# A planned graph-attention and GGNN kernel: seven durations in the plan's cost table are edited

## The chip, the cores and the metric

The kernel runs on one core of one Trainium2 chip. The metric is the device time of one execution in microseconds, as a median over the executions shown. TensorE (PE), VectorE (DVE), ScalarE (ACT), GpSimd (POOL) and the DMA queue of SyncE (SP) each run their own list of instructions; semaphores hold an instruction back until what it needs is done.

## What is computed

The input is x of 128 graphs x 128 nodes x 256 features, with an adjacency matrix of 128 x 128 for each graph. Four residual layers follow each other. The first three are graph attention (GAT), the last is a gated graph network of three steps (GRU):

```python
h = relu(layernorm(x))
# layers 0, 1, 2
Wh = h @ W
e = leaky_relu((Wh @ a1)[:, :, None] + (Wh @ a2)[:, None, :], 0.2)
att = softmax(where(adj > 0, e, -9e15))
x = x + elu(att @ Wh)            # layer 2: times nodemask ahead of elu
# layer 3, three steps i
m = h @ weight[i]
aggr = A.T @ m                   # A = (adj != 0)
h = gru_cell(aggr, h, w_ih, w_hh, b_ih, b_hh)
x = x + h
```

## The kernel before

**Groups.** The 128 graphs are cut into 33 groups: group 0 and group 32 have two graphs, the others four, so that a tile of a group is 128 partitions x 512 columns. A group passes through three attention layers and then through three GRU steps. While PE works on the GRU steps of group g, the attention layers of groups g+1 to g+3 are in progress, so that their long chains of DVE, ACT, POOL and DMA work lie beside matmuls of another group.

**Matmuls.** All are in float32, and the trace shows two MATMUL records for each product (transposes have one). An attention layer has the products `ahp` (L627: weights times nodes, four of 128 columns for each of two halves) and `hp` (L646, 256 columns). A GRU step has, for each half c of the features, products of 512 columns into four banks, `nn`, `r`, `z`, `ni` (L790): six from the state h and the recurrent weights, six from the aggregate `ag` and the combined weights. The aggregate itself is `agp` (L813: four products of 128 columns for each half k, from the node-major state `hn` and the adjacency `am`).

**Chains.** After `agp` of half k, ACT copies the bank to `ag` (L821), and the products of `ag` can start. After the last `r`, `ni` and `z` products of half c, ACT and DVE make the new state: tanh of r (L848), n (L851, L856), tanh (L858), d (L871 or L873, L877), h (L880). The next step's products read that h. For groups 2 to 30 the node-major copy `hn` of h is made with a DVE transpose (L476) and two DMA passes through DRAM (L479, L483); the others turn it on PE (`hnp`, L762, and an ACT copy, L802).

**Banks.** PSUM is dealt out in rings: two banks for `ahp` and `hp` (tag gat), five for the GRU products (gru), and one bank for `agp`, `hnp` and `hTp` (tag tr). An `agp` can thus begin only when ACT has copied out whatever was put into that single bank before it.

**What sets the order.** No order is written out by hand, and none is found at run time. Every operation is given to a planner (class Plan, L39 on) with an engine, a cost in microseconds and a rank (a due time in units of a group's third). The planner runs through the whole kernel once while it is built: an engine is free again when an operation's cost has passed, a result reaches another engine after a further LAG (0.26 from PE, 0.2 from DVE and ACT), a DMA lands after a time of its own, and a ring's slot comes free when its last user ends. At each step, for the engine that can start first, it takes from the operations that could start within WINDOW = 0.1 of the earliest the one of lowest rank. The result is one list for each engine, which the chip then executes in that order, whatever the true durations are:

```python
first = min(t for t, _ in found)
soon = [(op.rank, t, i) for i, (t, op) in enumerate(found) if t <= first + self.WINDOW]
_, t, i = min(soon)
```

The costs come from small functions: pe(cols) (L259), dve(cols) = 0.12 + cols/1000, act(cols) = 0.25 + cols/1400, and from numbers beside single operations. pe(128) is the cost of an `agp` or `ahp` product, that is of two MATMUL records. A cost is used by the planner alone: no instruction depends on it except through its place in its engine's list, and through the buffers that go with that order.

Of the kernel before, what the change touches and what calls it, by code (L numbers as in the profile page):

```python
# [14 lines left out]
P = 128  # L15
# [24 lines left out]
class Plan:  # L40
# [21 lines left out]
    def add(self, engine, cost, rank, fn, reads=(), writes=(), after=(), takes=()):  # L62


        reads = [k if isinstance(k, tuple) else (k, None) for k in reads]
        writes = [k if isinstance(k, tuple) else (k, None) for k in writes]
        vals = list(dict.fromkeys(v for v, _ in reads + writes))
        vals += [v for v in dict.fromkeys(takes) if v not in vals]
        op = Op(engine, cost, rank, fn, vals)
        for v in vals:  # L70
            v.ops.append(op)

        def others(book, key):
            for part, ops in book.get(key[0], {}).items():
                if part is None or key[1] is None or part == key[1]:
                    yield from ops

        for key in reads:
            for d in others(self.writers, key):
                op.deps[d] = True  # L80
        for key in writes:
            for book in (self.writers, self.readers):
                for d in others(book, key):
                    op.deps.setdefault(d, False)
        for d in after:
            op.deps.setdefault(d, False)
        for v, part in writes:
            w, r = self.writers.setdefault(v, {}), self.readers.setdefault(v, {})
            if part is None:
                w.clear()  # L90
                r.clear()
            else:
                r.pop(part, None)
            w[part] = [op]
        for v, part in reads:
            if (v, part) not in writes:
                self.readers.setdefault(v, {}).setdefault(part, []).append(op)
        for d in op.deps:
            d.users.append(op)
        self.ops.append(op)  # L100
        return op
# [84 lines left out]
def kernel(  # L186
# [25 lines left out]
    nc = tc.nc  # L212
    B, N, D = x.shape
# [44 lines left out]
        )  # L258

    def pe(cols):  # L260
        return 0.035 + cols / 600 if cols <= P else 0.01 + cols / 600

    def dve(cols):
        return 0.12 + cols / 1000
# [149 lines left out]
    def stats(xt, n, name, rank, takes):  # L414

        st = val(gw, "st", [G, 6], f"st_{name}", cut=n)
        mv = val(gw, "mv", [G, 2], f"mv_{name}", cut=n)
        nm = val(gw, "nm", [G], f"nm_{name}", cut=n)
        ve = val(gw, "ve", [G], f"ve_{name}", cut=n)
        rs = val(gw, "rs", [G], f"rs_{name}", bufs=3, cut=n)  # L420

        def one(b):
            add("DVE", dve(D), rank, lambda: nc.vector.bn_stats(st.t[:, b, :], xt.t[:, b, :]),
                reads=[(xt, b)], writes=[(st, b)], takes=[mv, nm, ve, rs, *takes])
            add("DVE", 0.13, rank, lambda: nc.vector.bn_aggr(mv.t[:, b, :], st.t[:, b, :]),
                reads=[(st, b)], writes=[(mv, b)])

        for b in range(n):
            one(b)
        add("DVE", 0.16, rank, lambda: nc.vector.tensor_scalar(  # L430
            nm.t, mv.t[:, :, 0], -1.0, None, op0=OP.mult), reads=[mv], writes=[nm])
        add("POOL", 0.3, rank, lambda: nc.gpsimd.tensor_scalar(
            ve.t, mv.t[:, :, 1], EPS, None, op0=OP.add), reads=[mv], writes=[ve])
        add("POOL", 1.04, rank, lambda: nc.gpsimd.tensor_tensor(
            rs.t, ve.t, mhalf[:, :n], op=OP.pow), reads=[ve], writes=[rs])
        return nm, rs
# [54 lines left out]
    def attention(g, l, xt, cap, xo):  # L491
# [5 lines left out]
        far = g >= FAR  # L497
# [6 lines left out]
                reads=[nm, rs], writes=[nm])  # L504

        def centred(b):
            add("ACT", 0.45, rank, lambda: nc.scalar.activation(  # L507
                xn.t[:, b, :], xt.t[:, b, :], AF.Relu, bias=nm.t[:, b : b + 1],
                scale=rs.t[:, b : b + 1] if far else 1.0,
            ), reads=[(xt, b), nm, *([rs] if far else [])], writes=[(xn, b)])  # L510


        def score(b, s):
            scr = val(gw, "scr", [D], f"scr_{name}_{b}_{s}")
            add("DVE", dve(D), rank, lambda: nc.vector.scalar_tensor_tensor(  # L515
                scr.t, xn.t[:, b, :], 1.0 if far else rs.t[:, b : b + 1], VA[l].t[:, s, :],
                op0=OP.mult, op1=OP.mult, accum_out=e.t[:, s, b : b + 1],
            ), reads=[(xn, b), rs, VA[l]], writes=[scr, (e, (s, b))])
# [53 lines left out]
            nmx.t, em.t, axis=AX.X, op=OP.max, negate=True), reads=[em], writes=[nmx])  # L572

        def power(b):
            add("ACT", 0.42, rank, lambda: nc.scalar.activation(  # L575
                em.t[:, b, :], em.t[:, b, :], AF.Exp, bias=nmx.t[:, b : b + 1],
                accum_out=sm.t[:, b : b + 1],
            ), reads=[(em, b), nmx], writes=[(em, b), (sm, b)])
# [4 lines left out]
        if l == 2:  # L583
            add("DVE", 0.16, rank, lambda: nc.vector.tensor_mul(
                ri.t, ri.t, nmT.t[:, FIRST[g] : FIRST[g] + n]), reads=[ri, nmT], writes=[ri])
        add("DVE", dve(n * P), rank, lambda: nc.vector.tensor_tensor(
            em.t, em.t, ri.t.rearrange("p (g o) -> p g o", o=1).to_broadcast([P, n, N]), op=OP.mult
        ), reads=[em, ri], writes=[em])

# [80 lines left out]
    def gat(g):  # L670
        b0, n = FIRST[g], SIZES[g]
        rank = 3.0 * g - lead(g)
        x0 = xt = val(grp, "x0", [G, D], f"x_{g}", cut=n)
        adj_t = val(grp, "adj", [G, N], f"adj_{g}", dtype=I32, cut=n)
        cap = val(grp, "cap", [G, N], f"cap_{g}", cut=n)
        am = val(grp, "am", [G, N], f"am_{g}", bufs=4, cut=n)
        load(128 * n, rank - 4, lambda: nc.sync.dma_start(
            x0.t, x[b0 : b0 + n].rearrange("b n d -> n b d")), writes=[x0])
        load(64 * n, rank - 3.6, lambda: nc.sync.dma_start(
            adj_t.t, adj[b0 : b0 + n].rearrange("b i j -> i b j")), writes=[adj_t])  # L680
        add("DVE", 0.42, rank, lambda: nc.vector.tensor_scalar(
            cap.t, adj_t.t, 0.0, 2.0 * BIG, op0=OP.is_gt, op1=OP.mult), reads=[adj_t], writes=[cap])
        add("DVE", 0.42, rank, lambda: nc.vector.tensor_scalar(
            cap.t, cap.t, -BIG, None, op0=OP.add), reads=[cap], writes=[cap])
        add("DVE", 0.42, rank + 1, lambda: nc.vector.tensor_scalar(
            am.t, adj_t.t, 0.0, None, op0=OP.not_equal), reads=[adj_t], writes=[am])
        for l in range(3):
            xo = val(grp, f"x{l + 1}", [G, D], f"xo_{g}_{l}", bufs=3 if l == 2 else 2, cut=n)
            attention(g, l, xt, cap, xo)
            xt = xo  # L690
        rank = 3.0 * g - lead(g) + 5.5
        hn = val(grp, "hn0", [G, D], f"hn_{g}_0", cut=n)

        F = KD * n * 32
        hT = val(grp, "h0", [Q, KD * G * 32], f"h_{g}_0")
        nm, rs = stats(xt, n, f"{g}_3", rank, [hn, hT])
        add("DVE", 0.16, rank, lambda: nc.vector.tensor_mul(nm.t, nm.t, rs.t),
            reads=[nm, rs], writes=[nm])

        def normed(b):  # L700
            add("ACT", 0.45, rank, lambda: nc.scalar.activation(
                hn.t[:, b, :], xt.t[:, b, :], AF.Relu, bias=nm.t[:, b : b + 1],
                scale=rs.t[:, b : b + 1],
            ), reads=[(xt, b), nm, rs], writes=[(hn, b)])

        for b in range(n):
            normed(b)

        def turned(k):

            ps = bank("tr", f"hTp_{g}_{k}")

            def turn(b):
                add("PE", 0.11, rank, lambda: nc.tensor.transpose(
                    ps.t[:, b * P : (b + 1) * P], hn.t[:, b, k * P : (k + 1) * P], ident
                ), reads=[(hn, b)], writes=[(ps, b)], takes=[hT])

            for b in range(n):
                turn(b)
            add("ACT", act(n * P), rank, lambda: nc.scalar.copy(  # L720
                hT.t[:, :, :F].rearrange("p q (k b c) -> p k b q c", k=KD, b=n)[:, k],
                ps.t[:, : n * P].rearrange("p (b q c) -> p b q c", b=n, q=Q),
            ), reads=[ps], writes=[(hT, k)])

        if g == 0:
            for k in range(KD):
                turned(k)
            return xt, am, hn, hT

        exchanged(  # L730
            [hn] * KD, lambda k: hn.t[:, :, k * P : (k + 1) * P], hT, f"h_{g}", n, rank
        )
        return xt, am, hn, hT
# [235 lines left out]
```

## Time and profile before

| | us |
|---|---|
| median of three executions | 2757.75 |
| lowest, highest | 2756.5, 2758.16 |
| the profiled execution, its own time | 2757.73 |
| span in the profile, first to last instruction | 2756.0 |
| PE busy (matmul records) | 2712.8 |
| DVE busy | 2082.3 |
| ACT busy | 1280.4 |
| POOL busy | 293.7 |

The profiled execution lies at the median of the three, and 1.7 us of its time lie outside the span. The mean granted clock of TensorE is 0.996 of full speed. Matmuls overlap in their pipeline, so that a record is longer than the distance to the next: a 128x512 matmul is recorded with 594 ns and followed by the next after 430 ns.

### The profile page before, as it was taken

Reading aid. Unit: us, or ns where it says so; the run is one execution under the profiler, and the core shown is the slowest. Engines: PE = TensorE matmul, PEld = TensorE weight load, DVE = VectorE, ACT = ScalarE, POOL = GpSimd, SP = SyncE. Lnnn points to the kernel's source line nnn. Section 1 sums busy time; section 2 is a strip of 40 time slices with the busy share of each in tenths; the row PEclk is TensorE's granted clock in tenths of the full one; section 3 lists DMA queues with packets and bytes.
Section 4 is the critical chain, followed back from the end, with each engine's and each line's share of the span. In section 5 each row is a group of like instructions: output and inputs, shape, how many; then the busy total and the mean of one; then the engine's idle time right before and its main releaser. Section 6 shows DMA issues by size and latency. Waiting matters only on the chain.

```text
span 2756.0 us, 32248 instructions
## 1 busy us (share of the span) xinstructions
PE 2712.8 (98%) x9563; PEld 1569.7 (57%) x9563; DVE 2082.3 (76%) x5541; ACT 1280.4 (46%) x2709; POOL 293.7 (11%) x369
## 2 busy tenths in 40 slices
PE   7899999999999999999999999999999999999998
PEld 4755555555555555555555555555555555555546
DVE  7778888778768887877788687778768886876643
ACT  4545444444444454444454445444444444444433
POOL 1111110101101101110111111111101010100000
PEclk9999999999999999999999999999999999999999
DMA  3113334433324433333333344323334333333310
GB/s 91 51 58 100 88 95 101 111 94 86 97 80 108 108 99 78 101 91 96 105 97 83 87 105 104 109 75 91 97 88 110 103 93 86 94 74 93 79 44 12
DMA packets 503094, 245.30 MB, mean 89 GB/s; under 512 B 280580, under 2 KB 472068, under 8 KB 502919
## 3 DMA queue, kind: packets, MB, share of 16 engines
q1 hardware_dynamic: 502918, 243.25, 33.5%
q8 instruction: 76, 1.25, 0.2%
q14 instruction: 100, 0.81, 0.1%
HBM read 139.28 MB, written 103.87 MB: 88 GB/s over the span
## 4 chain that ended last, share of the span: by engine, by line
PE 88%; DVE 8%; ACT 2%; DMA 1%; issue 1%; POOL 0%; SPq 0%; DVEq 0%; ACTq 0%; POOLq 0%
PE z L790 21%; PE r L790 21%; PE hp L646 11%; PE ni L790 11%; PE nn L790 10%; PE ahp L627 6%; PE agp L813 5%; DVE em L557 1%; DVE scr L515 1%; DVE xo L662 1%; DVE xo L664 1%; DVE d L877 1%; ACT em L575 1%; DVE h L880 1%; DVE n L856 0%
## 5 line engine op out<-in xcount | busy, mean ns | idle before, releaser
L790 PE MATMUL nn<-h,whh 128*128 128x512 f32 (+1 forms) x792 | 395.6, 581 | 1.9 <-DVE h L880 1.9
L790 PE MATMUL r<-ag,wc 128*128 128x512 f32 (+1 forms) x792 | 395.2, 581 | 1.3 <-ACT ag L821 1.3
L790 PE MATMUL ni<-ag,wc 128*128 128x512 f32 (+1 forms) x792 | 394.4, 579 | 1.4 <-ACT ag L821 1.4
L790 PE MATMUL z<-ag,wc 128*128 128x512 f32 (+1 forms) x792 | 394.2, 579 | 0.0
L790 PE MATMUL z<-h,whh 128*128 128x512 f32 (+1 forms) x792 | 394.2, 579 | 0.0
L790 PE MATMUL r<-h,whh 128*128 128x512 f32 (+1 forms) x792 | 394.2, 579 | 0.0
L851 DVE SCALAR_TENSOR_TENSOR n<-r,wn 128x512 f32<-128x512 f32 (+1 forms) x198 | 132.6, 670 | 336.5 <-ACT r L848 336.0
L646 PE MATMUL hp<-w,ah 128*128 128x256 f32 x1536 | 373.2, 381 | 0.5 <-ACT ah L634 0.2
L646 PEld LDWEIGHTS hp<-w,ah 128*128 128x128 f32 x1536 | 290.1, 190 | 131.4 <-issue 95.7
L515 DVE SCALAR_TENSOR_TENSOR scr<-xn,va 128x256 f32<-128x256 f32 x732 | 266.4, 423 | 33.9 <-ACT xn L507 33.6
L848 ACT ACTIVATE r<-r,brz 128x512 f32<-128x512 f32 (+1 forms) x198 | 133.2, 673 | 284.3 <-PE r L790 282.0
L813 PEld LDWEIGHTS agp<-am,hn 128*128 128x128 f32 x1536 | 202.3, 191 | 85.7 <-issue 73.5
L790 PEld LDWEIGHTS ni<-ag,wc 128*128 128x128 f32 x792 | 149.8, 190 | 177.9 <-issue 171.0
L790 PEld LDWEIGHTS r<-h,whh 128*128 128x128 f32 x792 | 149.3, 190 | 169.4 <-issue 162.8
L790 PEld LDWEIGHTS z<-h,whh 128*128 128x128 f32 x792 | 148.7, 190 | 168.3 <-issue 158.3
L821 ACT COPY ag<-agp 128x512 f32<-128x512 f32 (+1 forms) x198 | 113.0, 571 | 263.2 <-PE agp L813 262.8
L790 PEld LDWEIGHTS z<-ag,wc 128*128 128x128 f32 x792 | 148.4, 190 | 142.4 <-issue 138.2
L575 ACT ACTIVATE em<-em,nmx 128x128 f32<-128x128 f32 x384 | 149.4, 391 | 168.2 <-DVE nmx L571 166.4
L790 PEld LDWEIGHTS r<-ag,wc 128*128 128x128 f32 x792 | 146.1, 190 | 135.4 <-issue 120.5
L627 PEld LDWEIGHTS ahp<-at,xn 128*128 128x128 f32 x1536 | 191.3, 195 | 49.4 <-issue 37.6
L813 PE MATMUL agp<-am,hn 128*128 128x128 f32 x1536 | 205.3, 275 | 6.4 <-ACT hn L802 3.9
L526 POOL TENSOR_SCALAR xo<-xo 128x1024 f32<-128x1024 f32 (+1 forms) x66 | 73.2, 1110 | 1215.6 <-DVE xo L664 989.8
(94 smaller groups left out, 3474.1 us busy)
## 6 DMA issues: line engine op xcount, KB each, us to landing
d_hn<-tr_hn SPq DMA_DIRECT2D x116, 256.0 KB, 2.4
hn<-d_hn SPq DMA_DIRECT2D x464, 64.0 KB, 2.3
er<-de SPq DMA_DIRECT2D x90, 256.0 KB, 3.9
d_at<-tr_at SPq DMA_DIRECT2D x90, 256.0 KB, 2.0
at<-d_at SPq DMA_DIRECT2D x360, 64.0 KB, 2.0
x<-in_x_dram SPq DMA_DIRECT2D x31, 512.0 KB, 4.4
d_h<-tr_h SPq DMA_DIRECT2D x31, 512.0 KB, 2.9
h<-d_h SPq DMA_DIRECT2D x124, 128.0 KB, 3.1
```

The lines of the kernel that those rows point to most:

```text
L515: add("DVE", dve(D), rank, lambda: nc.vector.scalar_tensor_tensor(scr.t, xn.t[:, b, :], 1.0 if far else rs.t[:, b : b + 1], VA[l].t[:, s, ...
L526: add("POOL", 0.14 + n * D / 1070, rank, lambda: nc.gpsimd.tensor_scalar(xo.t, xt.t, 1.0, -1.0, op0=OP.mult, op1=OP.add), reads=[xt], writ ...
L557: add("DVE", dve(P) + (0.15 if far else 0.05), rank, lambda: nc.vector.scalar_tensor_tensor(em.t[:, b, :], e2_row(b), e.t[:, 0, b : b + 1] ...
L575: add("ACT", 0.42, rank, lambda: nc.scalar.activation(em.t[:, b, :], em.t[:, b, :], AF.Exp, bias=nmx.t[:, b : b + 1], accum_out=sm.t[:, b ...
L627: add("PE", pe(P), rank, lambda: nc.tensor.matmul(summed(ps, b), xn.t[:, b, k * P : (k + 1) * P], turned_weights(b), start=True, stop=True ...
L646: add("PE", pe(D), rank, lambda: nc.tensor.matmul(hp.t[:, b * D : (b + 1) * D], ah.t[:, k, c * P : (c + 1) * P], W[l].t[:, k, :], start=(k ...
L662: add("DVE", dve(T), rank, lambda: nc.vector.scalar_tensor_tensor(u(), hp.t, 0.0, u(), op0=OP.max, op1=OP.add), reads=[hp, *parts], writes ...
L790: nc.tensor.matmul(o, w.t[:, k, c * P : (c + 1) * P], m, start=start, stop=stop)
L813: nc.tensor.matmul(ps.t[:, b * P : (b + 1) * P], s, am.t[:, b, :], start=True, stop=True)
L821: add("ACT", act(TG), quick, lambda: nc.scalar.copy(t.t[:, :TG], ps.t[:, :TG]), reads=[ps], writes=[t])
L848: add("ACT", act(TG) + 0.1, quick, lambda: nc.scalar.activation(r.t[:, :TG], pr.t[:, :TG], AF.Tanh, bias=brz.t[:, cr : cr + 1], scale=0.5) ...
L851: add("DVE", dve(TG), quick, lambda: nc.vector.scalar_tensor_tensor(n.t[:, :TG], r.t[:, :TG], 1.0, wn.t[:, :TG], op0=OP.add, op1=OP.mult), ...
```

## The change

Seven places in the cost table get other numbers. Nothing is added, removed or resized: the same operations are planned, by the same rule.

```diff
     def pe(cols):
-        return 0.035 + cols / 600 if cols <= P else 0.01 + cols / 600
+        return 0.009 + cols / 600 if cols <= P else 0.01 + cols / 600
...
-            add("DVE", 0.13, rank, lambda: nc.vector.bn_aggr(mv.t[:, b, :], st.t[:, b, :]),
+            add("DVE", 0.08, rank, lambda: nc.vector.bn_aggr(mv.t[:, b, :], st.t[:, b, :]),
...
-            add("ACT", 0.45, rank, lambda: nc.scalar.activation(
+            add("ACT", 0.55, rank, lambda: nc.scalar.activation(
                 xn.t[:, b, :], xt.t[:, b, :], AF.Relu, bias=nm.t[:, b : b + 1],
...
-            add("DVE", dve(D), rank, lambda: nc.vector.scalar_tensor_tensor(
+            add("DVE", dve(D) + (0.03 if far else 0.13), rank, lambda: nc.vector.scalar_tensor_tensor(
                 scr.t, xn.t[:, b, :], 1.0 if far else rs.t[:, b : b + 1], VA[l].t[:, s, :],
...
-            add("ACT", 0.42, rank, lambda: nc.scalar.activation(
+            add("ACT", 0.55, rank, lambda: nc.scalar.activation(
                 em.t[:, b, :], em.t[:, b, :], AF.Exp, bias=nmx.t[:, b : b + 1],
...
-        add("DVE", dve(n * P), rank, lambda: nc.vector.tensor_tensor(
+        add("DVE", dve(n * P) + 0.1, rank, lambda: nc.vector.tensor_tensor(
             em.t, em.t, ri.t.rearrange("p (g o) -> p g o", o=1).to_broadcast([P, n, N]), op=OP.mult
...
-            add("ACT", 0.45, rank, lambda: nc.scalar.activation(
+            add("ACT", 0.55, rank, lambda: nc.scalar.activation(
                 hn.t[:, b, :], xt.t[:, b, :], AF.Relu, bias=nm.t[:, b : b + 1],
```

In the order of the lines, these are: the PE products of 128 columns (aggregates and attention), the aggregation of layernorm statistics (L425), the normalization on ACT in the attention layers (L507), the score products on DVE (L515; `far` is true for groups 2 and up), the exponentials (L575), the softmax's division (L586), and the normalization ahead of the GRU (L701).

## The prediction

> **What bounds the kernel now.** I read the page first: busy shares, the slices and the chain that ended last.
>
> ```profile
> PE 2712.8 (98%) x9563; PEld 1569.7 (57%) x9563; DVE 2082.3 (76%) x5541; ACT 1280.4 (46%) x2709; POOL 293.7 (11%) x369
> ...
> PE   7899999999999999999999999999999999999998
> ...
> PE 88%; DVE 8%; ACT 2%; DMA 1%; issue 1%; POOL 0%; SPq 0%; DVEq 0%; ACTq 0%; POOLq 0%
> ```
>
> PE carries the chain, and only the first two slices and the last show it less than nine tenths busy. Since records overlap, I price matmuls by the distance from one start to the next, read in the timeline of a stretch without waits (start, duration, engine and line, names, count):
>
> ```profile
> 1130.83 1.02 PE L790 MATMUL r<-h,whh 128*128 128x512 f32 x2
> 1131.68 1.05 PE L813 MATMUL agp<-am,hn 128*128 128x128 f32 x8
> 1132.58 1.02 PE L790 MATMUL nn<-h,whh 128*128 128x512 f32 x2
> 1133.44 1.02 PE L790 MATMUL r<-h,whh 128*128 128x512 f32 x2
> ```
>
> A product of 512 columns (two records) takes 0.858 us, one of 128 columns 0.895/4 = 0.223; likewise 256 columns take 0.431. All 9563 matmuls by these distances come to 2686 us. The profiled execution's span is 2756, so 70 us are lost to waits and to a slow clock. By laying these distances beside the true starts I find where: 50 us by 390 us, 6 us from there to 2465 us, 14 us in the tail. Here is a stretch of three groups (start:end, then busy time with count for PE, PEld, DVE, ACT, POOL; clock; DMA):
>
> ```profile
> 600.00:850.00 250.00, 249.81 (x867) 142.02 (x866) 195.48 (x516) 118.04 (x247) 27.45 (x33) 1.00 0.36 95
> ```
>
> So in the middle PE has practically no gap. A new order can win little there; it can lose, if it puts a matmul directly behind work that it must wait for. What such a spot costs, before shows at groups 2 and 3, here at group 3 (in brackets: idle time and releaser):
>
> ```profile
> 342.23 1.05 PE L813 MATMUL agp<-am,hn 128*128 128x128 f32 x8
> ...
> 343.32 0.58 ACT L821 COPY ag<-agp 128x512 f32<-128x512 f32 x1 [1.06 <-PE agp L813]
> ...
> 343.96 1.12 PE L790 MATMUL ni<-ag,wc 128*128 128x512 f32 x2 [0.68 <-ACT ag L821]
> ...
> 345.33 1.13 PE L790 MATMUL nn<-h,whh 128*128 128x512 f32 x2 [0.25 <-DVE h L880]
> ```
>
> `agp` takes its 0.895 and would be followed at 343.12; the product that reads its copy starts at 343.96: 0.84 us lost. ACT was free: this is the bare way from PE through the 0.58 copy and back. The next product waits for h: it would start at 344.82 and starts at 345.33, 0.52 more. The same 0.84 stands at 257.8 (`ni` behind `agp`), at 193.38, 2666.1 and 2690.3 (`agp` behind `hnp`, whose bank it needs).
>
> **What the Trainium skill says.** "PSUM — Partial Sum Buffer", Engine vs sequencer instructions: matmuls start and complete in program order. The stop at 343.12 agrees: nothing behind `ni` went ahead, though products of h were next. "Perfetto Trace Analysis", Optimizing Tensor Performance, says independent matmul groups should rotate through PSUM banks so that a copy lies beside the next group's matmuls; the tag tr has one bank, and 193.38 shows the price. The same page, Identifying the Most-Contended Engine, warns that matmul busy time is no measure of distance to the roof; here the 27 us between 2712.8 and 2686 are of that kind. "TensorE: Matmul & The Clock Gate", Part 1, says that an idle window of about 3.4 us halves the clock. The trace agrees (0.55 between 65 and 70 us, where PE idles); stops of 0.84 us left it at 1.00.
>
> **The change part by part.** No instruction is added or removed, so the only effect is on order.
>
> *Are the new durations the measured ones?* pe(128) becomes 0.222: it is 0.223 by distance, better than 0.248. The aggregation's 0.08 agrees (0.066 to 0.081 from start to start). But successive exponentials start 0.385 us apart (1380.58, 1380.98, 1381.36) and normalizations 0.49; 0.42 and 0.45 were nearer than 0.55, which are about the recorded lengths with their pipeline. Scores of far groups start 0.35 apart, and go from 0.376 to 0.406. The planner thus sees PE faster by 48 products x 0.026 = 1.2 us a group, and ACT slower by 12 exponentials x 0.13 + 16 normalizations x 0.10 = 3.2 us. It will plan PE closer to its suppliers.
>
> *The middle.* I compared the instruction lists of both builds. Before repeats every three groups, after every two. For each producer and first consumer I summed the PE distances of what stands between. After, around groups 14 and 15, PE has (merged):
>
> ```
> z  <-h_14_1_1
> agp_15_0_0  (last of its four)
> agp_14_2_0  x4
> agp_14_2_1  x4
> r  <-ag_14_2_0
> ...
> z  <-h_15_0_0
> agp_15_1_0  x4
> ni <-ag_15_1_0
> nn <-h_15_0_1
> ```
>
> Twice an `agp` stands directly behind another that fills the one tr bank, and once `ni` directly behind its `agp`. The first two recur in each even group from 6 to 28 (12 x 2), the third in each odd group from 5 to 29 (13): 37 stops with no work between. Before has none of them after 350 us; its smallest distance for `ag` there is 0.86. Ahead of 350 us there are four such stops before and five after (set-up apart), the last four groups have the same ones in both. 38 x 0.84 = +31.9 us, all on the path, since PE is the bound, takes matmuls in order, and no later slack gives time back.
>
> *Waits that follow.* After the third stop comes `nn` <-h_15_0_1. From the end of the last r product: tanh ends at 0.89, n (L851) 1.61, n (L856) 2.33, tanh 3.09; on DVE two scores and one mask step stand between and end at 3.5; then d, d, h until 5.6. PE has 5.18 of products between and the 0.84 stop: 6.02. No second wait, where group 3 before had 0.52 (1.7 us of softmax work and a transpose stood between instead). For `nn` <-h_14_1_1 there are 4.10 us behind the last `ni`, and the chain needs 0.2 + 0.69 + two steps of another group's mask (1.15) + 3 x 0.72 = 4.2: 0.1 x 12 = +1.2. That is an extrapolation: bound it by 0 and 0.52 each. The `hn` of 15_1_1 lands some 12.5 us behind r, by 6.3 for h and its transpose, 2.4 for the write and 1.5 + 2.2 for four reads; PE comes at 13.75. That is covered by 1.2 us, less than a slow landing takes (4.37 us for the write at 1343 cost PE 0.55). I take 0, bound +3 in sum.
>
> *Waits that go.* Before has 0.35 seven times (`r` 0.86 behind `agp`, in every third group), 0.55 at 1351 and 1.35 at 2511: -4.4.
>
> *SP and POOL.* Their issues follow their producers in both lists. In after the write of `at` for group 16 goes ahead of the reads of `hn` 15_1_1, but they wait for a landing until 8.7 us anyway: 0. POOL's work keeps its place ahead of L503 and L662: 0; were it late, the attention chain has over 45 us of PE work as cover (42 before).
>
> *Start.* PE stops there for the attention chain of groups 0 and 1. Summing DVE distances up to milestones, group 0's second layer comes 5 us later in after, group 1's second layer 3 us earlier, the first GRU step's states 1 us earlier. With opposite signs I take 0, bounds -5 and +5.
>
> Sum: 2757.73 + 31.9 + 1.2 - 4.4 = 2786.4 for the profiled execution. It equals the median within 0.02, so **2786** for the median.
>
> **Rivals.**
> *More than bare stops.* Every estimate above assumes ACT and DVE ready. If `nn` waits another 0.5 in 13 odd and 12 even groups (+11 in place of 1.2) and some DMA lands late (+3): 2799. For it: DVE is 76% busy and group 3's 0.52. Against: DVE's list has shorter work between in after.
> *Nothing measurable.* PE works off the same 2686 us, and each stop takes the place of another wait: 2757 +- 5. Against it: before has only 6 us of waits in the middle to be replaced.
> *It doesn't do what it says, or the lists mislead:* the new figures are partly lengths, not occupancies, as said; the effect is in the list either way.
> *Faster, by the start.* 46 us are lost by 390 us behind the first load. Its longest idles, 6.79 (`atp` waits at 70.25), 3.22 (56.57) and 3.63 (95.17), make 13.6, and the slow clock between 55 and 80 about as much again. If the earlier second layer of group 1 closed all of this, -27, the stops would still leave 2759. To end below 2752 the start must save over 34 us, three quarters of its loss; at 40 saved it gives 2746.
>
> **How the numbers follow.** Bare stops (forecast): 0.72, own range 2776 to 2796 by the start's bounds and the follow-up waits. More than bare stops: 0.20, up to 2802. Nothing measurable: 0.04. Faster by the start: 0.04. About 0.2% (5.5 us) is what a measurement can tell from no change. Slower: 0.92, same 0.04, faster 0.04. The range 2776 to 2802 takes the first two cases.
>
> **What would show it.** In the waits of PE, `agp` behind ACT `ag` (L821) should come from nothing to some 17 us (24 stops, each 0.68 as the trace counts it), `ni` behind `ag` from 1.4 to about 10. PE's busy time in a stretch of 250 us falls from 249.8 to some 247, and two groups take about 168.5 us where three took 249.2. DVE's and ACT's busy sums stay. I am wrong if those waits are absent, if they exceed 1 us each, or if the span's difference arises ahead of 390 us.

## The result, and the profile after

| | before | after |
|---|---|---|
| median, us | 2757.93 (4 runs beside those of after) | 2795.62 (4 runs, 2792.2 to 2797.64) |
| ratio | | 1.0134 [1.0121, 1.0147] |
| profiled execution: time, span | 2757.73, 2756.0 | 2792.2, 2790.4 |

After is slower by 1.34%, 37.7 us in the medians. Its profiled execution happens to be the fastest of its four; against it the difference is 34.5 us. The same three lines of the page, now of after (busy times; PE in 40 slices; shares of the chain that ended last):

```profile
PE 2727.0 (98%) x9563; PEld 1575.0 (56%) x9563; DVE 2087.5 (75%) x5541; ACT 1274.5 (46%) x2709; POOL 275.5 (10%) x369
...
PE   7999999999999999999999999999999999999998
...
PE 93%; DVE 3%; ACT 2%; DMA 2%; issue 1%; SPq 0%; POOL 0%; DVEq 0%; ACTq 0%; POOLq 0%
```

Nothing here tells of a loss. PE's share of the span is the same 98%, the slices are full, and the chain has even more PE in it. The page is too coarse for stops of a microsecond. The waits of PE over the whole run name them (us in total, times, longest):

```profile
PE agp L813 <- ACT ag L821: 17.3, 25, 1.1
PE ni L790 <- ACT ag L821: 10.1, 15, 0.7
```

So does the busy time of the stretch that had 249.81 us of PE in before:

```profile
600.00:850.00 250.00, 245.93 (x834) 137.46 (x833) 189.46 (x489) 112.64 (x239) 24.38 (x31) 1.00 0.35 92
```

Here are the two kinds of stop in the timeline of after. First `ni` behind its own `agp`, in group 11, with the copy on ACT and the end of the chain that makes `h` on DVE:

```profile
1016.95 0.69 DVE L871 TENSOR_TENSOR d<-h,n 128x512 f32<-128x512 f32 x1
1016.95 1.05 PE L813 MATMUL agp<-am,hn 128*128 128x128 f32 x8
...
1018.04 0.59 ACT L821 COPY ag<-agp 128x512 f32<-128x512 f32 x1 [0.45 <-PE agp L813]
1018.39 0.69 DVE L880 SCALAR_TENSOR_TENSOR h<-d,n 128x512 f32<-128x512 f32 x1
1018.68 1.12 PE L790 MATMUL ni<-ag,wc 128*128 128x512 f32 x2 [0.68 <-ACT ag L821]
...
1019.64 0.59 PE L790 MATMUL nn<-h,whh 128*128 128x512 f32 x1
```

Four `agp` products take 0.895, so `ni` could have started at 1017.84; it starts at 1018.68, 0.84 later. But look one line on: `nn` follows after 0.96 where products otherwise follow after 0.858. Its `h` had been done at 1019.08, so this is no wait for data: the first product behind a stop itself takes 0.10 more, and its record is 1.12 instead of 1.02. A stop costs 0.94. The other kind is `agp` behind `agp`, which needs the one bank of the tag tr; again the 0.10 shows, since 1.00 lies between the two starts and not 0.895:

```profile
971.10 1.16 PE L813 MATMUL agp<-am,hn 128*128 128x128 f32 x8 [0.68 <-ACT ag L821]
972.10 1.02 PE L790 MATMUL r<-ag,wc 128*128 128x512 f32 x2
```

To see where the time went, I laid the start-to-start distances of all products beside the true starts, as in the prediction. The loss is what a start lies behind its place; "middle" runs from the first GRU product of group 4 (near 400 us) to that of group 29 (near 2500 us). Other waits are those over 0.15 us, and "small" is the rest, with the 0.10 behind each stop:

| loss in us | start | stops of 0.84 | other waits | small | middle in all | tail |
|---|---|---|---|---|---|---|
| before | 49.6 | 0 | 3.0 | 2.7 | 5.7 | 10.6 |
| after | 49.1 | 30.1 | 2.6 | 7.4 | 40.2 | 10.8 |

All of the difference lies in the middle, in 36 stops (the 37th is in group 29, at the edge of the tail).

### The profile page after: what moved, and what is told of

Same layout as the page of the kernel before. It is cut to its first block, busy times and chain, and to the rows that moved or that the text cites. A ratio compares the mean times of both kernels' runs of the same rounds, so it can differ in the third digit from the quotient of the medians.

```text
span 2790.4 us, 32091 instructions
## 1 busy us (share of the span) xinstructions
PE 2727.0 (98%) x9563; PEld 1575.0 (56%) x9563; DVE 2087.5 (75%) x5541; ACT 1274.5 (46%) x2709; POOL 275.5 (10%) x369
## 4 chain that ended last, share of the span: by engine, by line
PE 93%; DVE 3%; ACT 2%; DMA 2%; issue 1%; SPq 0%; POOL 0%; DVEq 0%; ACTq 0%; POOLq 0%
PE r L790 22%; PE z L790 22%; PE ni L790 11%; PE hp L646 11%; PE nn L790 11%; PE agp L813 6%; PE ahp L627 6%; ACT ag L821 1%; DMA hn<-d_hn 1%; PE wcp L380 1%; DVE scr L515 1%; DMA d_hn<-tr_hn 0%; SPq L483 0%; PE ab L297 0%; DVE em L557 0%
## 5 line engine op out<-in xcount | busy, mean ns | idle before, releaser
L790 PE MATMUL ni<-ag,wc 128*128 128x512 f32 (+1 forms) x792 | 395.3, 581 | 10.1 <-ACT ag L821 10.1
L790 PE MATMUL nn<-h,whh 128*128 128x512 f32 (+1 forms) x792 | 396.1, 582 | 3.2 <-DMA h<-d_h 3.0
L790 PE MATMUL r<-h,whh 128*128 128x512 f32 (+1 forms) x792 | 394.2, 579 | 0.0
L790 PE MATMUL z<-ag,wc 128*128 128x512 f32 (+1 forms) x792 | 394.2, 579 | 0.0
L790 PE MATMUL z<-h,whh 128*128 128x512 f32 (+1 forms) x792 | 394.0, 579 | 0.0
L790 PE MATMUL r<-ag,wc 128*128 128x512 f32 (+1 forms) x792 | 392.3, 580 | 0.0
L646 PE MATMUL hp<-w,ah 128*128 128x256 f32 x1536 | 358.8, 381 | 0.2 <-ACT ah L634 0.2
L851 DVE SCALAR_TENSOR_TENSOR n<-r,wn 128x512 f32<-128x512 f32 (+1 forms) x198 | 133.0, 672 | 253.2 <-ACT r L848 252.9
L515 DVE SCALAR_TENSOR_TENSOR scr<-xn,va 128x256 f32<-128x256 f32 x732 | 295.8, 453 | 35.1 <-ACT xn L507 34.9
L790 PEld LDWEIGHTS z<-h,whh 128*128 128x128 f32 x792 | 150.3, 190 | 176.9 <-issue 171.5
L790 PEld LDWEIGHTS ni<-ag,wc 128*128 128x128 f32 x792 | 147.4, 190 | 168.9 <-issue 149.9
L843 ACT ACTIVATE wn<-nn,bh 128x512 f32<-128x512 f32 (+1 forms) x198 | 133.5, 674 | 233.7 <-PE nn L790 230.4
L790 PEld LDWEIGHTS r<-h,whh 128*128 128x128 f32 x792 | 148.3, 190 | 159.8 <-issue 153.8
L790 PEld LDWEIGHTS z<-ag,wc 128*128 128x128 f32 x792 | 148.6, 190 | 157.1 <-issue 154.5
L813 PE MATMUL agp<-am,hn 128*128 128x128 f32 x1536 | 212.0, 279 | 24.6 <-ACT ag L821 17.3
L790 PEld LDWEIGHTS r<-ag,wc 128*128 128x128 f32 x792 | 144.7, 190 | 132.5 <-issue 126.0
L662 DVE SCALAR_TENSOR_TENSOR xo<-hp,xo 128x512 f32<-128x512 f32 x192 | 124.3, 679 | 114.1 <-ACT t L660 113.6
```

What stands on the lines that cost most here:

```text
L515: add("DVE", dve(D) + (0.03 if far else 0.13), rank, lambda: nc.vector.scalar_tensor_tensor(scr.t, xn.t[:, b, :], 1.0 if far else rs.t[:, ...
L646: add("PE", pe(D), rank, lambda: nc.tensor.matmul(hp.t[:, b * D : (b + 1) * D], ah.t[:, k, c * P : (c + 1) * P], W[l].t[:, k, :], start=(k ...
L662: add("DVE", dve(T), rank, lambda: nc.vector.scalar_tensor_tensor(u(), hp.t, 0.0, u(), op0=OP.max, op1=OP.add), reads=[hp, *parts], writes ...
L790: nc.tensor.matmul(o, w.t[:, k, c * P : (c + 1) * P], m, start=start, stop=stop)
L813: nc.tensor.matmul(ps.t[:, b * P : (b + 1) * P], s, am.t[:, b, :], start=True, stop=True)
L843: add("ACT", act(TG) + 0.1, quick, lambda: nc.scalar.activation(wn.t[:, :TG], nn.t[:, :TG], AF.Identity, bias=bh.t[:, cn : cn + 1]), reads ...
```

## The experiments

Ten kernels, each timed in three rounds beside before (medians of before 2757.96 to 2758.73). Where a diff has `move`, a product or copy is taken out of the finished order and put ahead of (0) or behind (1) a named one, so the rest of the order stays as the planner made it. The numbers of the loss are of the profiled execution of each.

**Are the stops the cause? Remove a third, remove all, add them to before.** In after, the last `agp` product of an odd group's step 0 stood apart from its other three, directly ahead of the next block. The first kernel puts it back behind the three; the second does this too and puts products into the other two stops of the pattern. The third starts from before and puts `ni` directly behind its `agp` in step 2 of groups 5 to 29:

```diff
+        for g in range(6, 29, 2):
+            move([("agp", g + 1, 0, 0, 3), ("ag", g + 1, 0, 0)], ("agp", g + 1, 0, 0, 2), 1)
```

> The changed kernel's order with 12 small moves: the last of the four products of agp for half 0 of step 0 of each odd group from 7 to 29 is put directly behind the other three, with its ACT copy behind it, so that nine products of 0.858 us stand between it and the next user of the single tr bank. Bare stops (the forecast's mechanism): 12 stops fewer, 12 x 0.84 = -10.1 us, 2785.5. If late data or engine load set the time rather than the stops: within 3 us of the changed kernel's 2795.6. If the stop only moves to the next wait: the second agp stop of the pair grows, no gain.

```diff
+        for g in range(6, 29, 2):
+            move([("agp", g + 1, 0, 0, 3), ("ag", g + 1, 0, 0)], ("agp", g + 1, 0, 0, 2), 1)
+            move([("agp", g, 2, 0, b) for b in range(4)] + [("ag", g, 2, 0)], ("nn", g, 2, 1, 1), 0)
+        for g in range(5, 30, 2):
+            move([("nn", g, 1, 1, 0)], ("ni", g, 1, 0, 0), 0)
```

> As e1, and the other two kinds of stop are filled too: agp for half 0 of step 2 of each even group goes ahead of three products, and one product of nn goes between agp and ni in step 1 of each odd group. All 37 stops of the middle have at least 0.85 us of matmuls in them. Bare stops: -37 x 0.84 = -31.1 us, 2764.5, with the waits for hn (3.7 us in the profile of the changed kernel) and the start as they are. If the order costs more than its stops (late hn, DVE and ACT queues): 2775 or more. If the stops took the place of other waits: little gain, 2785 to 2795.

```diff
+        for g in range(5, 30):
+            move([("ag", g, 2, 0), ("ni", g, 2, 0, 0)], ("agp", g, 2, 0, 3), 1)
```

> The kernel before with the suspected cost put in: in step 2 of groups 5 to 29 the first product of ni that reads ag is put directly behind the agp whose copy it needs (in the list before, 2.57 us of matmuls or 0.86 lie between). All costs in the plan are those of before, so no engine's load or due time changes. Bare stops: 25 x 0.84 = +21.0 us, 2778.9. If it needs the denser plan to cost anything (late suppliers): 2758 to 2762. If a stop drags a second wait behind it (0.5 each): 2791.

| | median, us | ratio to before | middle in all | stops of 0.84 | other waits |
|---|---|---|---|---|---|
| after, a third removed | 2781.9 (2775.42 to 2784.72) | 1.0081 [1.0066, 1.0096] | 27.1 | 20.1 | 2.0 |
| after, all taken apart | 2763.21 (2758.34 to 2767.41) | 1.0018 [1.0011, 1.0025] | 12.2 | 0 | 7.2 |
| before with 25 stops | 2782.5 (2780.16 to 2782.82) | 1.0084 [1.0067, 1.0101] | 27.7 | 20.1 | 2.5 |

The stops go and come as placed. In the waits of PE from 390 to 2465 us, of the kernel with a third removed:

```profile
PE ni L803 <- ACT ag L834: 8.1, 12, 0.7
PE agp L826 <- ACT ag L834: 7.4, 11, 0.7
```

and of before with the stops put in:

```profile
PE ni L803 <- ACT ag L834: 15.5, 23, 0.7
```

The last gives the price most cleanly, since hardly anything else moved: the middle grows from 5.7 to 27.7, 22.0 us by the 24 stops in it, 0.92 each. The kernel without stops keeps 6.5 us more than before in the middle. Its waits there are all for transfers but one of 0.3:

```profile
PE agp L829 <- DMA hn<-d_hn: 3.0, 6, 1.1
PE ahp L643 <- DMA at<-d_at: 1.6, 3, 0.6
```

That PE comes to these transfers earlier, now that the stops are gone, is the likely reason; it was not tested. So 28.0 us of the middle are gone with the stops, of the 34.5 by which after had more than before.

**Which edit brings the stops?** One alone on before (L507, the normalization of the attention layers), then the last one alone (L701), and the six others without it:

```diff
-            add("ACT", 0.45, rank, lambda: nc.scalar.activation(
+            add("ACT", 0.55, rank, lambda: nc.scalar.activation(
                 xn.t[:, b, :], xt.t[:, b, :], AF.Relu, bias=nm.t[:, b : b + 1],
```

> The kernel before with one of the seven edits alone: the normalization of the attention layers at 0.55 in place of 0.45. Its instruction list has stops worth about 23 us between 350 and 2480 us where before has none (11 pairs of agp behind agp, and a handful at groups 4 to 6). Bare stops: +23 less before's 4.4 us of waits that may go, plus up to 4 of late hn: 2776 to 2781. If the edits add up by what they do to the planned load, one of seven should cost a part, some +5 to +10: 2763 to 2768.

```diff
-            add("ACT", 0.45, rank, lambda: nc.scalar.activation(
+            add("ACT", 0.55, rank, lambda: nc.scalar.activation(
                 hn.t[:, b, :], xt.t[:, b, :], AF.Relu, bias=nm.t[:, b : b + 1],
```

> The kernel before with only the normalization of L701 at 0.55 instead of 0.45. Theory (stops are a property of the whole list and don't add up over the edits; this list has none of them, and `nn` stands at least 7.77 us behind the last `r` product that its state needs): within the scatter of before, 2753 to 2762. Rival (each edit has its share, and this one's, without which the six others ran at 2751.82, is some 40 us): 2790 or more.

The six others are after with this last line at 0.45:

> Six of the seven edits, without the one of the normalization ahead of the GRU. The list has 2 stops ahead of 390 us and none behind it. Counted stops: +2, and the start like that of the changed kernel or of before: 2755 to 2762. If each edit has its own share of the loss: about 2790. If planned PE and ACT loads are what makes the order bad: 2780 or more.

L507 alone took 2785.02 (2783.26 to 2785.91), ratio 1.0095 [1.008, 1.011], 4.0 us above the span that I gave, which left out the 0.10 behind each stop. Its waits in the middle are mainly 25 of one kind:

```profile
PE agp L813 <- ACT ag L821: 16.9, 25, 0.7
```

L701 alone took 2763.49 (2760.04 to 2768.18, 20 runs), 1.0019 [1.0012, 1.0026]: 5 us above before and 1.5 above the span that I gave, with no stop. The six others took 2751.82 (2749.16 to 2755.04, 11 runs), 0.9978 [0.9969, 0.9987], faster than before and 3.2 below the span. So "the edit at fault" doesn't exist: leaving L701 out saves 43.8 us, and putting it in alone costs 4.8 against before beside it. Counted in the built lists between 350 and 2540 us, where after has 37 stops and before none, a single edit brings 27 (L507), 10 (the products' cost), 4 (the aggregation) or 0 (each of the others). With one edit left out there are 37 (the division), 26 (the products' cost), 15 (the aggregation), 14 (the scores), 13 (L507), 6 (the exponentials) and 2 (L701). The counts don't add up: each cost shifts which operation the planner takes next, and the pattern then repeats from group to group.

What L701 alone does lose is another wait, in every third group, which no count of stops can see. Its profiled execution took 2768.07, the second longest of the 20, so that this profile shows more loss than the median has:

```profile
PE nn L790 <- DVE h L880: 9.8, 8, 2.0
```

**A miss: six edits without the products' cost.** This list has 26 stops.

```diff
-        return 0.009 + cols / 600 if cols <= P else 0.01 + cols / 600
+        return 0.035 + cols / 600 if cols <= P else 0.01 + cols / 600
```

> Six of the seven edits, without the one of the products of 128 columns. The list has 26 stops (ni directly behind its agp, in every group) between 390 and 2465 us. Counted stops at 0.93 us each (0.84 and some 0.09 of a slower restart, as the run with 25 inserted stops shows): +24, 2782, give or take 5 for the start. If the planned speed of PE is what makes the order bad: 2757 to 2762. If each edit has its own share of the loss: about 2790.

It took 2809.94 (2807.35 to 2811.64), ratio 1.0189 [1.0173, 1.0204], worse than after with fewer stops. The waits of PE in the middle:

```profile
PE ni L790 <- ACT ag L821: 16.2, 24, 0.7
PE nn L790 <- DVE h L880: 9.8, 48, 0.3
```

The second line looks small: 9.8 us. The distances say more. From one product's start to the next, half of the 48 places lose 0.48 (with the 0.10 of the stop just ahead) and half 0.36, 20.2 us in all; the trace counts as idle only what passes the end of the record before. The timeline of group 10 shows why `h` is late:

```profile
934.95 1.02 PE L790 MATMUL r<-ag,wc 128*128 128x512 f32 x2
...
936.25 0.40 ACT L575 ACTIVATE em<-em,nmx 128x128 f32<-128x128 f32 x1 [5.60 <-DVE nmx L571]
...
936.65 0.67 ACT L848 ACTIVATE r<-r,brz 128x512 f32<-128x512 f32 x1
...
940.13 0.68 DVE L871 TENSOR_TENSOR d<-h,n 128x512 f32<-128x512 f32 x1
...
941.57 0.69 DVE L880 SCALAR_TENSOR_TENSOR h<-d,n 128x512 f32<-128x512 f32 x1
...
942.32 1.13 PE L790 MATMUL nn<-h,whh 128*128 128x512 f32 x2 [0.22 <-DVE h L880]
```

From the start of the last `r` product to the end of `h` it is 7.31 us here. In after, around 1016, it is 6.42 (1012.66 to 1019.08), and PE's list has the same 6.04 us of products ahead of that `nn` in both. The 0.89 is ACT's and DVE's order: an exponential of another group stands ahead of the tanh of `r`, which starts 1.70 behind the product instead of 1.12. That is 0.58; the rest comes on the way through DVE, where layernorm statistics (L425) stand ahead of L851, and two mask steps (L681, L683) rather than one ahead of L871. My expectation had counted the stops and not looked at this chain.

To test this, one product per group that doesn't need the late state was put ahead of the waiting one:

```diff
+        for g in range(5, 30):
+            move([("nn", g, 1, 1, 0)], ("nn", g, 1, 0, 1), 0)
```

> The kernel with six of the seven edits (the cost of the 128-column products left as it was), with one product per group moved: the `nn` product of the second half with the first old state, which doesn't need the late state, stands ahead of the `nn` product that waited 0.48 us for `h` in groups 5 to 28 of that kernel's run (2809.94 us). The 26 stops for the `ag` copy stay. Theory (the excess over the stops is a second wait per group, and it is a question of distance in the list: 6.04 us from the last `r` product to the waiting `nn` there, where the chain of tanh, DVE steps and `h` took 7.36; now 6.90 and a stop of 0.94): these waits go, 24 x 0.48 = 11.5 us, so about 2798, and the 0.36 us waits of step 2 stay. Rival (a wait taken away in one place comes back in another, or the excess is the start's): about 2810.

It took 2799.32 (2798.22 to 2800.52), ratio 1.0151 [1.0135, 1.0166]: 10.6 us less. Half of the waits are gone, as the waits in the middle show, while the stops stayed:

```profile
PE ni L803 <- ACT ag L834: 16.9, 25, 0.7
PE nn L803 <- DVE h L895: 4.8, 24, 0.4
```

**A second miss of the same kind: group 2 planned earlier.** To win back what after loses at the first GRU step of group 2 (below), its lead was raised:

```diff
-    LEADS = [9.0, 9.5, 7.0, 6.5, 7.0]
+    LEADS = [9.0, 9.5, 8.0, 6.5, 7.0]
```

> The changed kernel with one more edit: the lead of group 2 is 8.0 in place of 7.0, so that its attention is due earlier. Its list has 21.6 us of matmuls between group 2's last attention product and its first GRU product, where the changed kernel has 15.6 and before 20.3, and 26 stops in the middle in place of 37. If PE's loss at group 2's first GRU step (9 us between 210 and 235 us in the changed kernel, 2.5 in before) is a matter of that distance, it falls to 3 or less; with 11 stops fewer at 0.93: 2795.6 - 6 - 10 = 2779, and the runs lie closer together. If that loss has another cause: 2785.

It took 2795.83 (2793.3 to 2798.61), ratio 1.0137 [1.012, 1.0154], like after. The start did gain: its loss is 42.8 against 49.1, and PE is busy for the whole of 210 to 235 us. (The expectation gives before a loss of 2.5 us there; its profile shows PE busy for all 25 us at full clock, so 0.) But the whole list behind it changed too. It has the 26 stops expected (25 of them, 21.0 us, in the middle), and the 48 waits of `nn` for `h` besides (`PE nn L790 <- DVE h L880: 9.9, 48, 0.3` in its waits); the middle comes to 52.0. As before, the expectation had counted stops alone.

**Start-to-start distances instead of recorded lengths.** The prediction says that the new durations are partly lengths. Here the plan gets distances:

```diff
@@ L507, L701
-            add("ACT", 0.55, rank, lambda: nc.scalar.activation(
+            add("ACT", 0.5, rank, lambda: nc.scalar.activation(
@@ L515
-            add("DVE", dve(D) + (0.03 if far else 0.13), rank, lambda: nc.vector.scalar_tensor_tensor(
+            add("DVE", dve(D) + (-0.03 if far else 0.03), rank, lambda: nc.vector.scalar_tensor_tensor(
@@ L575
-            add("ACT", 0.55, rank, lambda: nc.scalar.activation(
+            add("ACT", 0.39, rank, lambda: nc.scalar.activation(
@@ L586
-        add("DVE", dve(n * P) + 0.1, rank, lambda: nc.vector.tensor_tensor(
+        add("DVE", dve(n * P), rank, lambda: nc.vector.tensor_tensor(
```

> The plan given the distances from one start to the next, as the profile of before shows them, in place of recorded lengths: exponentials 0.39, normalizations 0.50, scores 0.346 (far) and 0.406, products and aggregations as in the changed kernel, division as before. One stop at 338 us and none behind it. Counted stops: 2755 to 2762. If a plan that is closer to the chip gains by itself: below 2750. If denser plans lose: 2775 or more.

It took 2753.27 (2750.38 to 2756.24, 13 runs), ratio 0.9983 [0.9974, 0.9991]: a little faster than before, and 1.7 below the span that I gave. Its middle loses 3.4 us, and so does that of the six edits, against 5.7 in before. Both are faster than before by about 0.2%, with intervals that end below 1. That the better figures are the reason is not shown: the six edits without L701 keep the long exponentials, and do as well.

## Why the prediction was right, and what it had too small

It forecast 2786, with 2776 to 2802 as the range; the median is 2795.6. The cause is the one named: stops in PE's list, shown by removing them, by adding them to before, and by the waits. The waits it said would show it came as said: 17.3 (some 17) and 10.1 (about 10). The size was less good: 28.3 us forecast, 37.7 measured in the medians, near the upper end of the range. By its own steps, for the profiled execution (28.7 us predicted, 34.2 measured between the two loss sums):

- **38 stops of 0.84: +31.9.** All 37 beyond 350 us are there, each 0.84 to the hundredth. What the price left out is the 0.10 behind each. In the profile of before it could be read: the quoted record of `ni` at 343.96 is 1.12 long where others are 1.02. The wait for `h` in the next line hid it. Small losses in the middle rose from 2.7 to 7.4: 4.7 us, of which 36 x 0.10 = 3.6 are this.
- **Waits that go: -4.4.** This step failed. Before's own went, the 1.35 in the tail among them, but the other waits of the middle came to 2.6 after 3.0, so only 0.4 was won there. In their place stands the wait for `hn` that the prediction had called covered, with 0 and a bound of +3. PE comes to the `agp` of step 2 in the odd groups about when the reads land:

```profile
1056.80 1.02 PE L790 MATMUL nn<-h,whh 128*128 128x512 f32 x2
1057.99 1.13 PE L813 MATMUL agp<-am,hn 128*128 128x128 f32 x8 [0.17 <-DMA hn<-d_hn]
```

  `agp` would have started at 1057.66, so 0.33 is lost and only 0.17 of it shows as idle. Seven such places, at 0.18 to 0.51 each, and one of another `agp` (0.38) sum to 2.6 us. The prediction took 2.2 us for a read to land. But the list of the DMA queue had changed too, which it priced at 0: in after the read of a later group's x (L677, 512 KB) is issued directly ahead of these reads, in all eleven such places from 550 to 2241 us. Of the queue, around the same `agp`:

```profile
1049.10 0.38 SPq L479 DMA_DIRECT2D d_hn<-tr_hn  x1
1051.61 0.39 SPq L677 DMA_DIRECT2D x<-in_x_dram  x1
1052.09 2.38 SPq L483 DMA_DIRECT2D hn<-d_hn  x4
```

  In after's trace the 29 reads of `hn` issued within 2.5 us behind a read of x, and with a recorded landing, land 4.2 us after their issue in the median, the 263 others 2.3. In before none stands so, and the median of its 290 is 2.3. Moving the read of x was not tried.
- **Waits that follow: +1.2.** Neither came. `nn` <-h_15_0_1 was rightly priced at 0: group 11's `h` is done at 1019.08, 0.56 ahead of its product. `nn` <-h_14_1_1 didn't wait either, so 0.
- **Start: 0, bounds 5.** Right in the sum, and by luck. By 210 us after is 5 us ahead. From there to 235 us, at group 2's first GRU step, it loses 8 us where before loses nothing, and before gives the rest back by 400, in four waits that after lacks (0.77 of `ahp`, and 0.47, 1.26 and 0.52 of `nn` and `agp`). After's list puts that step nearer to the normalization it reads: 8.6 us of products lie between the attention's last product of group 2 and the first `agp`, where before has 19.4. The prediction compared the DVE milestones, which had come earlier, and not how much earlier PE now asks for them. In the timeline of PE:

```profile
214.91 0.61 PE L813 MATMUL agp<-am,hn 128*128 128x128 f32 x4
216.39 0.98 PE L813 MATMUL agp<-am,hn 128*128 128x128 f32 x4 [0.88 <-ACT hn L701]
218.46 2.07 PE L813 MATMUL agp<-am,hn 128*128 128x128 f32 x8 [1.08 <-ACT ag L821]
...
229.89 1.13 PE L790 MATMUL nn<-h,whh 128*128 128x512 f32 x2 [2.97 <-DMA h<-d_h]
```

- **The profiled execution stands for the median.** For before it did, within 0.2; for after it lies 3.4 below. The start varies: the kernels with a third of the stops removed and with all of them apart have the same list as after up to 390 us, and lost 54.3 and 46.8 us there where after's profile shows 49.1. The granted clock, as the mean of a whole execution, goes with the time: in after 2792.2 and 2794.28 had 0.996, 2796.96 and 2797.64 had 0.994; with a third removed, 2775.42 had 0.997, 2780.29 had 0.996, and 2783.51 and 2784.72 had 0.994.

Terms: 28.7 + 4.7 (behind the stops) + 4.0 (waits that go) - 1.2 (waits that follow) - 1.3 (start, with the stop counted there) - 0.6 (the tail, with the stop at its edge counted there and the 1.35 under the waits that go) = 34.3.

Of the rivals, "more than bare stops" was nearer in size than the forecast (2799; its 25 waits of 0.5 make 12.5 and not 11, so 2801) and wrong in mechanism for this list: what it feared, `nn` waiting some 0.5 for `h` in every group, after doesn't have; two of the experiments do. "Nothing measurable" fails: the difference is 37.7 us, and before had only 3.0 us of other waits in the middle to be replaced. "Faster, by the start" fails: the start's loss is 49.1 after 49.6. The rival that the new figures are lengths is true of the figures: the plan with distances has one stop and no more than the time of before.

## What to carry to other kernels

In a list that one full engine works off in order, compare the built lists before you run them: for each producer and its first consumer on that engine, sum the distances of what stands between, and look for those near zero; one such place in a pattern that repeats in 24 groups is worth 22 us. Then do the same for the long chains through other engines, with the order of *their* lists, since a wait for one exponential and one mask step more cost as much here as the stops did. Look at the DMA queue's list as well, for a large read that now stands ahead of a small one that PE waits for. A cost table that is nearer to the recorded durations needn't give a better order. Whether start-to-start distances are the better input isn't shown here, so judge each new table by its list: no edit's effect could be read from that of another.

## What the runs showed of the hardware

The record of an operation isn't the time that it holds its engine. Three normalizations of L507 from 1096.78 in after's profile are merged to 1.58 us, where one is recorded with 0.59 to 0.60: each further one adds 0.49. The Trainium skill, "ScalarE: Activation LUTs", What ACT_TABLE_LOAD costs, agrees: back-to-back activations overlap by about 93 ns there, and an estimate from it, 0.59 - 0.093, is 0.50. The table's 0.55 for L507 lies between distance and length; the old 0.45 was about as far below the distance as 0.55 is above it.

The clock fell without a single idle of 3 us. After the two waits of 0.88 and 1.08 quoted above, the granted clock (third number from the end) of three stretches of one microsecond, in after, was:

```profile
217.00:218.00 1.00, 0.37 (x2) 0.18 (x2) 1.00 (x2) 1.00 (x3) 0.00 (x0) 1.00 0.23 72
218.00:219.00 1.00, 0.54 (x2) 0.55 (x3) 0.93 (x3) 1.00 (x3) 0.00 (x0) 0.67 0.00 0
219.00:220.00 1.00, 1.00 (x7) 1.00 (x6) 1.00 (x2) 0.89 (x2) 0.00 (x0) 0.50 0.00 0
```

The microsecond from 218 has 0.67, so the fall to half speed came at about 218.34 (an estimate from the 1.00 and 0.50 beside it). The next ones show 0.50, 0.50, 0.63 and, from 222 on, 1.00, although PE is busy all the time from 219 on. From 215 to 218 PE worked 1.49 of 3 us (0.51, 0.61 and 0.37). So two waits close together slow the products behind them, which the stops of 0.84 did not do in the repeating groups (1.00 over 390 to 2465 us). The Trainium skill, "TensorE: Matmul & The Clock Gate", What's actually happening, speaks of an idle window of about 3.4 us; here no idle was above 1.1, and the measurement decides.

Nor does the length of a single wait decide. In the kernel with L701 alone, the wait of 2.02 for `h` that ended at 1688.79 was followed by 0.53, 0.50, 0.50 and 0.76 in the microseconds from 1689; in after the 2.97 that ended at 229.89 left the clock at 1.00. Which rule does decide isn't shown. In the clock records of after's trace the falls ahead of the tail stand at 57.91, 68.15, 92.04 and 218.34, which are 3, 7 and 37 times 3.41 us apart: it may matter where a wait lies in a fixed grid.

Of the two kernels with the same start, the one with a third of the stops removed had half speed from 220.5 as well, and once more from 230.8 to about 237.7, behind a wait of 3.6 for `h`. From the products' distances that cost about 3 us, of the 5.2 by which its start lost more than after's: that is part of why the start varies.
